# A two-layer graph network on one core: all seven column pieces of the first pass in fp32r, with GpSimd casting the last

## The chip, the cores and the metric

The kernel runs on one core of a Trainium2 chip. The metric is the device time of one execution in microseconds (us); 966.26 us is the median of three runs of the kernel before (964.35 to 967.14). Five engines work in parallel on the core, each through its own queue in program order: TensorE (PE in the profile, with PEld for its weight loads), VectorE (DVE), ScalarE (ACT), GpSimd (POOL) and SyncE (SP), which here issues most DMAs. Matmuls write to PSUM; all else lies in SBUF. fp32r is a 4-byte type that TensorE multiplies in one go[...].

## The reference

6250 nodes with 128 features each, 206,250 directed edges (100,000 drawn ones in both directions, and one loop per node), sorted by destination. Cut to what is computed:

```python
h = relu(layernorm(x))
feat = h * clip(out_degree, 1) ** -0.5
x = x + relu(segment_sum(feat[src], dst)) @ W0.T + b0            # first layer
h = relu(layernorm(x))
msg = h[src] @ W_msg.T + b_msg + edge_embed[edge_type]
x = x + gru_cell(segment_sum(msg, dst), h)                       # second layer
```

The two segment sums over edges are the bulk of it. All in float32.

## The kernel before, in words

**The idea.** The kernel does not gather rows. It builds the adjacency matrix (how many edges lead from each source to each destination) as small integers, exact in bf16, and takes each segment sum as a matmul of a node table with that matrix. Nodes are padded to 49 blocks of 128. The first pass (`by_matrix`, L757 to L909) builds the matrix in chunks of destination columns (`FRONT`: one of 128, then 24 of 256), uses each chunk at once for the first layer, and writes it to DRAM (`adj_d`). The second pass (L915 on) reads it back in columns of up to 512 for the second layer.

**The prologue** (L365 to L755) sorts edge data into windows by transposes and indirect DMAs on GpSimd's queue, takes layernorm statistics (`st`), counts degrees, and makes the table `tab1` of the first layer: seven pieces of seven source blocks each. A float32 table is split into terms that add up to it: piece 0 (`q < NARROW`) in three bf16 terms (`SPL`), the other six in two fp32r terms (`terms_of`, L722).

**The first pass**, one iteration of the loop at L856 for each chunk c, and one more at the end. An iteration does three things in turn, in 8 rounds of 32 columns (4 for the first chunk):
- *Building chunk c.* Every second round VectorE writes one-hot rows of 64 columns (`hots`: `hot_l`, `hot_c`, L334), one batch ahead of their use, in two buffers. Each round TensorE multiplies them (`ev`, L801, 32 small matmuls), and ScalarE copies the counts from PSUM into the chunk's matrix (`adj`, L810, two copies).
- *The sums of chunk c-1* (`sums`, L758; matmuls at L769): for each piece, block and term one matmul of 128x128 weights with 256 matrix columns. Piece 0 takes the bf16 matrix as it is: 7 blocks x 3 terms = 21 matmuls. Pieces 1 to 6 need the matrix in fp32r, so each is cast first (`cast`, L871): pieces 1, 3, 5 on ScalarE, 2, 4, 6 on VectorE, into three rotating buffers `wide1`; 6 x 7 x 2 = 84 matmuls. The 105 are spread over the 8 rounds (`ends`), 13 a round and 14 in the last. `cast_at` says in which round each cast is put: {0: (1, 2), 2: (3,), 3: (4,), 4: (5,), 5: (6,)}.
- *The dense end of chunk c-2* (`first_layer`, L815), a generator whose steps are taken in rounds 0, 2, 3 and 6: relu on ScalarE, the product with W0 on TensorE (L825), the residual sum on VectorE (L829, L830), statistics (L835, L836). Its last step, `late`, comes in round 2 of the next iteration: ScalarE's square root `rstd` (L838) and then VectorE's reciprocal and `sh` (L839, L840).

The order on TensorE, ScalarE and VectorE in this pass is the order of the program (`manual_schedule`, L786). GpSimd has no instruction in it.

The names that the steps below touch: `one_hot` L331, `hots` L341, `first_place` L361 (the memory of the first chunk's matrix, idle in the prologue, that also takes one early batch of one-hots), `st` L459, `tab1` L530, `inside` L623, `terms_of` L722, `sums` L758, `build` L790, `first_layer` L815, the loop L846 to L909.

Of the kernel before, what the change touches and what calls it, by code (L numbers as in the profile page):

```python
# [10 lines left out]
F32 = mybir.dt.float32  # L11
BF16 = mybir.dt.bfloat16
F32R = mybir.dt.float32r
# [3 lines left out]
ALU = mybir.AluOpType  # L17
# [4 lines left out]
P = 128  # L22
N = 6250
NB = 49
NP = NB * P
H = 128
# [5 lines left out]
CB = 7  # L32
NCH = NB // CB
# [3 lines left out]
HALF = P // 2  # L37
WP = 125
WB = 25
ROWS = 3  # L40
GB = 4
# [4 lines left out]
DC = 2 * P  # L46
FRONT = [(0, P)] + [(d, DC) for d in range(P, NP, DC)]
HP = 7
SPL = 3
LEVELS = 4  # L50
BY_ACT = (0, 2, 4, 6)
NARROW = 1
BACK = [(0, 3 * P)] + [(d, min(4 * P, NP - d)) for d in range(3 * P, NP, 4 * P)]


def spread(n, k):

    return [n * (i + 1) // k for i in range(k)]
# [200 lines left out]
def by_matrix(  # L259
# [22 lines left out]
    nc = tc.nc  # L282
# [70 lines left out]
    def run(steps, n):  # L353
        for _ in range(n):
            if next(steps, "end") == "end":
                return
# [4 lines left out]
    first_place = adj_odd.tile([P, NB, DC], BF16, name="adj").rearrange("p n d -> p (n d)")  # L361
# [3 lines left out]
    with tc.tile_pool(name="pro", bufs=1) as pro, tc.manual_schedule(engines={mybir.EngineType.DVE}):  # L365
# [90 lines left out]
            nc.vector.tensor_scalar(row, row, float(4 * HALF), None, op0=ALU.mult)  # L456


        st = pro.tile([P, NB, 6], F32, name="st")  # L459
        stats_left = iter(range(NB))  # L460

        def stats(n):
# [25 lines left out]
        for k0 in range(0, NT // P + 1, 4):  # L488
            k1 = min(k0 + 4, NT // P + 1)
            n = min(P, NT - k0 * P)  # L490
            for i, given in enumerate((dst_f, code_b, typ_b, low_b)):
                ps = pps.tile([P, 4, P], F32, name="turn")
                for k in range(k0, k1):
                    n = min(P, NT - k * P)
# [30 lines left out]
        nc.sync.dma_start(out=flat[NT : NT + 1, :], in_=far)  # L525
        look.close()


        tab1_p = early.enter_context(tc.tile_pool(name="tab1_p", bufs=1, side="right"))
        tab1 = [  # L530
            tab1_p.tile([P, SPL, CB, H], BF16, name=f"tab1_{q}")
            if q < NARROW
            else tab1_p.tile([P, 2, CB, H], F32R, name=f"tab1_{q}")
            for q in range(NCH)
        ]
        look = ExitStack()
        wnd = look.enter_context(tc.tile_pool(name="wnd", bufs=2))
# [70 lines left out]
        def fetch(b0_, nb):  # L608

            got = wnd.tile([P, GB, ROWS, 4, HALF], I16, name="got")  # L610
            for b in range(nb):
                nc.gpsimd.indirect_dma_start(  # L612
                    out=got[:, b].rearrange("p r f j -> p (r f j)"),
                    out_offset=None,
                    in_=edges_flat,
                    in_offset=bass.IndirectOffsetOnAxis(ap=row_i[:, b0_ + b : b0_ + b + 1], axis=0),
                )
            typ_of[b0_] = wnd.tile([P, GB * WP], BF16, name="typ")
            w0_ = b0_ * WP
            turns_ = {i: pps.tile([P, 4, P], F32, name="turn") for i in (1, 0, 2)}  # L620
            n = nb * ROWS
            g = got[:, :nb].rearrange("p b r f j -> p (b r) f j")
            inside = wnd.tile([P, 2, GB * ROWS, HALF], BF16, name="inside", bufs=1)  # L623
            fields = wnd.tile([P, GB * ROWS, 3, 2, HALF], BF16, name="fields")
            for d in range(2):
                nc.vector.tensor_tensor(
                    inside[:, d, :n].rearrange("p a (j t) -> p a j t", t=2),
                    g[:, :, 0, :].rearrange("p a (j t) -> p a j t", t=2),
                    mine[d][:, b0_ * ROWS : b0_ * ROWS + n].unsqueeze(2).to_broadcast([P, n, HALF // 2, 2]),
                    ALU.is_equal,  # L630
                )
            for d in range(2):
                nc.vector.tensor_tensor(  # L633
                    fields[:, :n, :, d, :],
                    g[:, :, 1:, :],
                    inside[:, d, :n].unsqueeze(2).to_broadcast([P, n, 3, HALF]),
                    ALU.mult,
                )
            for i in (1, 0, 2):
                for b in range(nb):  # L640
                    for r in range(ROWS):
                        nc.tensor.matmul(  # L642
                            turns_[i][:, b, :],
                            fields[:, b * ROWS + r, i].rearrange("p d j -> p (d j)"),
                            ident_b,
                            start=(r == 0),
                            stop=(r == ROWS - 1),
                        )
            for i in (1, 0, 2):
                ws = turns_[i][:, :nb, :WP]  # L650
                if i == 1:
                    nc.scalar.copy(typ_of[b0_][:, : nb * WP].rearrange("j (b p) -> j b p", p=WP), ws)
                else:
                    to = (code_t, None, lo_t)[i][:, w0_ : w0_ + nb * WP, :]
                    nc.scalar.copy(
                        to.rearrange("j (b p) t -> j b p t", p=WP), ws.unsqueeze(3).to_broadcast([P, nb, WP, 2])
                    )
# [64 lines left out]
        def terms_of(c):  # L722
            f, tab = f_of.pop(c), tab1[c]
            nc.vector.tensor_scalar(tab[:, 0], f, 0.0, None, op0=ALU.max)
            if c < NARROW:
                nc.vector.scalar_tensor_tensor(f, f, 0.0, tab[:, 0], op0=ALU.max, op1=ALU.subtract)
                nc.vector.tensor_copy(tab[:, 1], f)
                nc.vector.tensor_tensor(tab[:, 2], f, tab[:, 1], ALU.subtract)
            else:
                nc.vector.scalar_tensor_tensor(  # L730
                    tab[:, 1], f, 0.0, tab[:, 0].bitcast(F32), op0=ALU.max, op1=ALU.subtract
                )

        for i in range(NCH):
            if i >= 3:
# [46 lines left out]
    with tc.tile_pool(name="adj_even", bufs=1, reuse_waits="tile") as adj_even, tc.tile_pool(  # L782
        name="wide1", bufs=3, reuse_waits="tile"
    ) as wide1p, tc.tile_pool(
        name="ev_ps", bufs=3, space=PSUM, reuse_waits="tile"
# [58 lines left out]


        RUN = 32  # L846
        cast_at = {0: (1, 2), 2: (3,), 3: (4,), 4: (5,), 5: (6,)}
        TOTAL = (NARROW * SPL + (NCH - NARROW) * 2) * HP
        ROUNDS = DC // RUN
        batches = [d // 2 for d in range(0, NP, 2 * TW)]  # L850
        ready = early_hots
        made = len(ready)
        adjs = {}
        before, late = None, iter(())
        NC = len(FRONT)
        for c in range(NC + 1):  # L856
            d0, nd = FRONT[c] if c < NC else (NP, 0)
            acc, steps = None, iter(())
            wide = {}
            if c > 0:  # L860
                done = adjs.pop(c - 1)
                n = FRONT[c - 1][1]
                acc, steps = sums(
                    n, tab1, lambda q, done=done, wide=wide: wide[q] if q >= NARROW else done[:, q * HP : (q + 1) * HP]
                )
            if c < NC:
                adjs[c] = (adj_even if c % 2 else adj_odd).tile([P, NB, DC], BF16, name="adj") if c > 0 else adj_first
            rounds = nd // RUN if c < NC else ROUNDS
            ends = spread(TOTAL, rounds)

            def cast(q):  # L871
                wide[q] = wide1p.tile([P, HP, DC], F32R, name="wide1")
                make = nc.scalar.copy if (q - NARROW) % 2 == 0 else nc.vector.tensor_copy
                make(wide[q][:, :, :n], done[:, q * HP : (q + 1) * HP, :n])  # L874

            for r in range(rounds):
# [15 lines left out]
                for q in casts:  # L892
                    if r > 0:
                        cast(q)
                if before is not None and r in (0, 2, 3, 6):
                    run(before, 1)
                if r == 2:
                    run(late, 1)
                run(steps, ends[r] - (ends[r - 1] if r else 0))
            run(steps, TOTAL)  # L900
            late = before if before is not None else iter(())
            before = first_layer(c - 1, acc) if acc is not None else None
            if c < NC:
# [212 lines left out]
```

## Time and profile before

| what | us |
|---|---|
| median of 3 runs | 966.26 |
| profiled execution, its own time | 970.11 |
| its span in the profile | 968.3 |
| prologue, until the first sums on TensorE | 117 |
| first pass, until the second pass's sums start | 117 to about 571 |
| second pass | 571 to 968 |
| PE busy, of the span | 886.2 (92%) |
| DVE busy | 807.8 (83%) |
| ACT busy | 739.8 (76%) |
| POOL busy | 35.9 (4%), all of it in the prologue |

The profile is of one execution. A line of the groups names line, engine, operation, output<-input, shape and count, then busy time and the mean duration of one in ns, then the idle time of the engine before them and who ended it. A line of the timeline gives start, duration, engine, line, operation, operands and how many instructions were merged. Busy time is a union: a DVE or ACT instruction begins a little before the one ahead has left the pipeline, so durations add up to more than the busy time, and what an instruction costs is best taken from start to start. The ends of matmuls are modelled.

### The profile page before, as it was taken

Reading aid. Unit: us, or ns where it says so; the run is one execution under the profiler, and the core shown is the slowest. Engines: PE = TensorE matmul, PEld = TensorE weight load, DVE = VectorE, ACT = ScalarE, POOL = GpSimd, SP = SyncE. Lnnn points to the kernel's source line nnn. Section 1 sums busy time; section 2 is a strip of 40 time slices with the busy share of each in tenths; the row PEclk is TensorE's granted clock in tenths of the full one; section 3 lists DMA queues with packets and bytes.
Section 4 is the critical chain, followed back from the end, with each engine's and each line's share of the span. In section 5 each row is a group of like instructions: output and inputs, shape, how many; then the busy total and the mean of one; then the engine's idle time right before and its main releaser. Section 6 shows DMA issues by size and latency. Waiting matters only on the chain.

```text
span 968.3 us, 25145 instructions
## 1 busy us (share of the span) xinstructions
PE 886.2 (92%) x11049; PEld 735.5 (76%) x11049; DVE 807.8 (83%) x898; ACT 739.8 (76%) x1407; POOL 35.9 (4%) x73
## 2 busy tenths in 40 slices
PE   4356499999999999999999989999999999999995
PEld 3334399899899999999999878777777777777774
DVE  6969988999999999999999788987887778766753
ACT  3167889999999999999999995767577666667552
POOL 3540000000000000000000000000000000000000
PEclk9677599999999999999999999999999999999998
DMA  9430245575576576576476679877676677565530
GB/s 267 137 96 18 53 130 168 163 207 170 157 206 175 152 206 180 148 206 186 142 206 191 178 260 315 267 250 250 229 256 230 231 260 245 200 227 209 183 88 20
DMA packets 200296, 180.65 MB, mean 187 GB/s; under 512 B 10353, under 2 KB 188583, under 8 KB 200023
## 3 DMA queue, kind: packets, MB, share of 16 engines
q1 hardware_dynamic: 197938, 172.72, 57.5%
q0 software_dynamic: 1664, 4.95, 1.7%
q8 instruction: 88, 1.44, 0.6%
q10 hardware_dynamic: 576, 1.29, 0.4%
q14 instruction: 30, 0.25, 0.1%
HBM read 95.07 MB, written 83.87 MB: 185 GB/s over the span
## 4 chain that ended last, share of the span: by engine, by line
PE 74%; DVE 11%; ACT 7%; DMA 5%; issue 2%; POOL 1%; another core or an unknown queue 0%; SPq 0%; DVEq 0%; ACTq 0%
PE acc L769 52%; PE ev L801 10%; DMA piece<-adj_d 4%; DVE leave L1011 3%; PE turn L642 2%; PE gate L972 2%; PE acc L825 2%; PE gate L973 2%; DVE wide L1038 2%; ACT wide L1031 1%; ACT adj L810 1%; PE sums L671 1%; ACT f L935 1%; PE msg_ps L964 1%; PE tr L953 1%
## 5 line engine op out<-in xcount | busy, mean ns | idle before, releaser
L769 PE MATMUL acc<-wide,tab 128*128 128x256 f32 (+2 forms) x3374 | 600.1, 329 | 3.5 <-DVE wide L1038 3.4
L769 PEld LDWEIGHTS acc<-wide,tab 128*128 128x128 f32 x3374 | 492.0, 189 | 68.2 <-issue 17.7
L810 ACT CAST adj<-ev 128x784 bf16<-128x784 f32 x392 | 298.9, 820 | 30.6 <-PE ev L801 27.6
L1031 ACT ACTIVATE wide<-piece 128x512 fp32r<-128x512 bf16 (+1 forms) x336 | 201.0, 601 | 70.0 <-PE acc L769 64.0
L334 DVE TENSOR_TENSOR hot_l<-lo_t,iota 128x4096 bf16<-128x4096 bf16 x97 | 221.6, 2285 | 0.6 <-PE ev L801 0.5
L1011 DVE TENSOR_REDUCE leave<-piece 128x7 f32<-128x3584 bf16 (+2 forms) x43 | 154.9, 3602 | 47.2 <-DMA piece<-adj_d 47.2
L874 ACT CAST wide<-adj 128x1792 fp32r<-128x1792 bf16 (+1 forms) x75 | 125.2, 1669 | 0.8
L801 PE MATMUL ev<-hot_c,hot_l 64*128 64x49 bf16 x6208 | 114.2, 182 | 7.4 <-DVE hot_c L334 4.2
L801 PEld LDWEIGHTS <-hot_l 64*128 64x128 bf16 x6208 | 93.0, 93 | 36.0 <-issue 8.9
L334 DVE TENSOR_TENSOR hot_c<-code_t,iota 128x1600 bf16<-128x1600 bf16 x97 | 95.5, 985 | 0.0
L1038 DVE CAST wide<-piece 128x3584 fp32r<-128x3584 bf16 (+2 forms) x43 | 82.3, 1921 | 10.4 <-PE acc L769 10.4
L874 DVE CAST wide<-adj 128x1792 fp32r<-128x1792 bf16 (+1 forms) x75 | 81.0, 1079 | 8.7 <-ACT adj L810 7.9
L769 PE MATMUL acc<-adj,tab 128*128 128x256 bf16 x525 | 67.2, 277 | 0.5 <-ACT adj L810 0.5
L1031 ACT ACTIVATION_READ_ACCUMULATOR wide<-piece 128x1 f32 x336 | 63.2, 188 | 0.0
L769 PEld LDWEIGHTS <-tab 128*128 128x128 bf16 x525 | 48.1, 99 | 8.1 <-issue 0.6
L949 ACT COPY sum_sb<-acc 128x512 f32<-128x512 f32 (+2 forms) x13 | 7.3, 562 | 37.4 <-PE acc L769 37.4
L642 PE MATMUL turn<-ident_b,fields 128*128 128x128 bf16 x225 | 20.9, 280 | 15.4 <-DVE fields L633 15.4
L642 PEld LDWEIGHTS <-fields 128*128 128x128 bf16 x225 | 19.9, 131 | 16.1 <-issue 14.0
L612 POOL DMA_INDIRECT got<-flat,row_i x25 | 26.4, 1058 | 23.5 <-DVE m_dve L667 13.6
L972 PE MATMUL gate<-hT,whh_sb 128*128 128x512 f32 (+2 forms) x52 | 25.4, 570 | 1.2 <-DVE hT L961 1.2
L973 PE MATMUL gate<-msg,wih_sb 128*128 128x512 f32 (+2 forms) x52 | 25.3, 567 | 0.0
L980 ACT ACTIVATE rg<-gate,brz 128x512 f32<-128x512 f32 (+2 forms) x13 | 8.6, 664 | 20.0 <-PE gate L973 20.0
(160 smaller groups left out, 558.2 us busy)
## 6 DMA issues: line engine op xcount, KB each, us to landing
adj_d<-adj SPq DMA_DIRECT2D x24, 3136.0 KB
piece<-adj_d SPq DMA_DIRECT2D x77, 896.0 KB
piece<-adj_d SPq DMA_DIRECT2D x14, 672.0 KB
piece<-adj_d SPq DMA_DIRECT2D x7, 448.0 KB
out_dram<-res SPq DMA_DIRECT2D x11, 256.0 KB
xs<-in_x_dram SPq DMA_DIRECT2D x6, 448.0 KB
adj_d<-adj SPq DMA_DIRECT2D x1, 1568.0 KB
flat<-turned SPq DMA_DIRECT2D x3, 512.0 KB
```

The lines of the kernel that those rows point to most:

```text
L334: nc.vector.tensor_tensor(to.rearrange("p j (k t) -> p j k t", t=2), twice.unsqueeze(2).to_broadcast([P, n, m // 2, 2]), of[:, :m].rearran ...
L612: nc.gpsimd.indirect_dma_start(out=got[:, b].rearrange("p r f j -> p (r f j)"), out_offset=None, in_=edges_flat, in_offset=bass.IndirectOf ...
L642: nc.tensor.matmul(turns_[i][:, b, :], fields[:, b * ROWS + r, i].rearrange("p d j -> p (d j)"), ident_b, start=(r == 0), stop=(r == ROWS ...
L769: nc.tensor.matmul(acc[:, : 2 * P].rearrange("f (t n) -> f t n", t=2) if twice else acc[:, :nd], tab[:, s, i, :], a[:, i, :P].unsqueeze(1) ...
L801: nc.tensor.matmul(ps[:, d, j * NB : (j + 1) * NB], hot_l[half, t, :], hot_c[half, t, :NB], start=True, stop=True,)
L810: nc.scalar.copy(adj[:, :, part * 16 : (part + 1) * 16].rearrange("p n (j d) -> p n j d", d=2), ps[:, :, : 8 * NB].rearrange("p d (j n) -> ...
L874: make(wide[q][:, :, :n], done[:, q * HP : (q + 1) * HP, :n])
L972: nc.tensor.matmul(ps[:, :nd], whh_sb[:, cols], hT[:, :nd], start=True, stop=False)
L973: nc.tensor.matmul(ps[:, :nd], wih_sb[:, cols], msg[:, :nd], start=False, stop=True)
L1011: nc.vector.tensor_reduce(leave[:, q * HP : (q + 1) * HP, c], piece, AX.X, ALU.add)
L1031: nc.scalar.activation(pieces[q][:, i, :nd], piece[:, i, :nd], AF.Copy, accum_out=leave[:, q * HP + i, c : c + 1],)
L1038: nc.vector.tensor_copy(pieces[q][:, :, :nd], piece[:, :, :nd])
```

## The change

All seven pieces of `tab1` become two fp32r terms, so a chunk's sums are 7 x 7 x 2 = 98 matmuls, all on a cast matrix. The casts: pieces 1, 3, 5 on ScalarE as before; 0, 2, 4 on VectorE; piece 6 on GpSimd, into a buffer of its own (`wide1_last`, one buffer). The sums of a chunk begin in round 1 instead of round 0, and the 13 matmuls left after round 7 are run in round 0 of the next iteration (`rest`). The steps of `first_layer` move from rounds 0, 2, 3, 6 to 1, 3, 4, 6. To make room in SBUF, `st` and `inside` of the prologue are placed in `first_place`.

On the engines' queues: in each iteration VectorE's three casts stand in rounds 0, 1 and 3 (before: 0, 3 and 5), ScalarE's in 0, 2 and 4 as before. GpSimd gets 25 casts (one of 128x896, 24 of 128x1792 elements) behind its last prologue DMA. Each waits for ScalarE's last copies of the chunk and, by its single buffer, for the `rest` matmuls in round 0. ScalarE's first `adj` copy of an iteration now waits also for GpSimd's cast of the iteration before, which reads the same matrix buffer. VectorE has two instructions fewer in the prologue (of the four that made piece 0's terms, two are left). SP's queue is the same.

```diff
-NARROW = 1
...
-        st = pro.tile([P, NB, 6], F32, name="st")
+        st = first_place.bitcast(F32)[:, NB * P - NB * 6 :].rearrange("p (b s) -> p b s", s=6)
...
         tab1 = [
-            tab1_p.tile([P, SPL, CB, H], BF16, name=f"tab1_{q}")
-            if q < NARROW
-            else tab1_p.tile([P, 2, CB, H], F32R, name=f"tab1_{q}")
+            tab1_p.tile([P, 2, CB, H], F32R, name=f"tab1_{q}")
             for q in range(NCH)
         ]
...
-            inside = wnd.tile([P, 2, GB * ROWS, HALF], BF16, name="inside", bufs=1)
+            inside = first_place[:, 2 * NB * (P - 6) - 2 * GB * ROWS * HALF : 2 * NB * (P - 6)]
+            inside = inside.rearrange("p (d a j) -> p d a j", d=2, j=HALF)
...
             nc.vector.tensor_scalar(tab[:, 0], f, 0.0, None, op0=ALU.max)
-            if c < NARROW:
-                nc.vector.scalar_tensor_tensor(f, f, 0.0, tab[:, 0], op0=ALU.max, op1=ALU.subtract)
-                nc.vector.tensor_copy(tab[:, 1], f)
-                nc.vector.tensor_tensor(tab[:, 2], f, tab[:, 1], ALU.subtract)
-            else:
-                nc.vector.scalar_tensor_tensor(
-                    tab[:, 1], f, 0.0, tab[:, 0].bitcast(F32), op0=ALU.max, op1=ALU.subtract
-                )
+            nc.vector.scalar_tensor_tensor(
+                tab[:, 1], f, 0.0, tab[:, 0].bitcast(F32), op0=ALU.max, op1=ALU.subtract
+            )
...
-        cast_at = {0: (1, 2), 2: (3,), 3: (4,), 4: (5,), 5: (6,)}
-        TOTAL = (NARROW * SPL + (NCH - NARROW) * 2) * HP
+        cast_at = {0: (0, 1, NCH - 1), 1: (2,), 2: (3,), 3: (4,), 4: (5,)}
+        TOTAL = NCH * 2 * HP
...
-        before, late = None, iter(())
+        before, late, rest = None, iter(()), iter(())
...
-                    n, tab1, lambda q, done=done, wide=wide: wide[q] if q >= NARROW else done[:, q * HP : (q + 1) * HP]
+                    n, tab1, lambda q, wide=wide: wide[q]
...
-            ends = spread(TOTAL, rounds)
+            ends = [0, *spread(TOTAL, rounds)]
 
             def cast(q):
-                wide[q] = wide1p.tile([P, HP, DC], F32R, name="wide1")
-                make = nc.scalar.copy if (q - NARROW) % 2 == 0 else nc.vector.tensor_copy
+                if q == NCH - 1:
+                    wide[q] = wide1p.tile([P, HP, DC], F32R, name="wide1_last", bufs=1)
+                    make = nc.gpsimd.tensor_copy
+                else:
+                    wide[q] = wide1p.tile([P, HP, DC], F32R, name="wide1")
+                    make = nc.scalar.copy if q % 2 else nc.vector.tensor_copy
                 make(wide[q][:, :, :n], done[:, q * HP : (q + 1) * HP, :n])
...
-                if before is not None and r in (0, 2, 3, 6):
+                if r == 0:
+                    run(rest, TOTAL)
+                if before is not None and r in (1, 3, 4, 6):
                     run(before, 1)
                 if r == 2:
                     run(late, 1)
                 run(steps, ends[r] - (ends[r - 1] if r else 0))
-            run(steps, TOTAL)
+            if c == NC:
+                run(steps, TOTAL)
+            rest = steps
```

## The prediction, on record before the run

> **What bounds the kernel now.** I read the page first (shares, then the span in slices), then busy times by stretch of the first pass, then the timelines of TensorE (PE) and VectorE (DVE) inside one iteration, and last GpSimd's (POOL's) groups and timeline, since the change gives that engine new work. Part 2 of the page:
>
> ```profile
> PE   4356499999999999999999989999999999999995
> DVE  6969988999999999999999788987887778766753
> ACT  3167889999999999999999995767577666667552
> POOL 3540000000000000000000000000000000000000
> ```
>
> The change lies in the first pass, slices 5 to 23 (117 to 571 us). There three engines are at nine tenths, and POOL has nothing. Which of the three ends last is read from one iteration (from its first build matmul to the next one's), and from 19 of them; the columns are PE, PEld, DVE, ACT, POOL busy, then the granted clock, DMA share and GB/s:
>
> ```profile
> 172.33:190.60 18.27, 18.27 (x367) 16.57 (x367) 17.23 (x20) 17.11 (x22) 0.00 (x0) 1.00 0.60 178
> 172.33:519.46 347.13, 347.13 (x6946) 314.77 (x6947) 327.48 (x362) 325.21 (x400) 0.00 (x0) 1.00 0.62 178
> ```
>
> 347.13 / 19 = 18.27 us for an iteration, all of it PE: TensorE never waits, at full clock. DVE has 18.27 - 17.23 = 1.04 us free, ScalarE 18.27 - 17.11 = 1.16. So the pass is bound by TensorE, with two engines 6% behind it. TensorE's timeline at the end of the pass shows what its two kinds of matmul cost with nothing between them:
>
> ```profile
> 510.69 1.82 PE L769 MATMUL acc<-wide,tab 128*128 128x256 f32 x13
> ...
> 556.47 2.45 PE L769 MATMUL acc<-adj,tab 128*128 128x256 bf16 x21 [0.54 <-ACT adj L810]
> 558.68 0.84 PE L769 MATMUL acc<-wide,tab 128*128 128x256 f32 x5
> ...
> 559.73 9.72 PE L769 MATMUL acc<-wide,tab 128*128 128x256 f32 x79
> ```
>
> A group's time holds the modelled tail of its last matmul (a median of 0.285 us for fp32r). From start to start, bf16 takes (558.68 - 556.47) / 21 = 0.105 us, fp32r (9.72 - 0.285) / 78 = 0.121. DVE's order in the iteration:
>
> ```profile
> 172.05 1.06 DVE L874 CAST wide<-adj 128x1792 fp32r<-128x1792 bf16 x1
> 173.03 2.28 DVE L334 TENSOR_TENSOR hot_l<-lo_t,iota 128x4096 bf16<-128x4096 bf16 x1
> 175.23 0.98 DVE L334 TENSOR_TENSOR hot_c<-code_t,iota 128x1600 bf16<-128x1600 bf16 x1
> 176.13 2.28 DVE L334 TENSOR_TENSOR hot_l<-lo_t,iota 128x4096 bf16<-128x4096 bf16 x1
> 178.34 0.98 DVE L334 TENSOR_TENSOR hot_c<-code_t,iota 128x1600 bf16<-128x1600 bf16 x1
> 180.23 0.17 DVE L839 RECIPROCAL rstd<-rstd 128x2 f32<-128x2 f32 x1 [0.91 <-ACT rstd L838]
> ```
>
> Two things are to be seen. Nearly all of DVE's free 1.04 us is one wait, 0.91 us for ScalarE's rstd. And the one-hot batches come just in time: the batch that ends at 176.21 is used by round 2's matmuls, which TensorE starts at 176.47, 0.26 us later. If DVE is later there, TensorE waits at once.
>
> **TensorE's part of the change.** 105 matmuls become 98: 21 bf16 go (21 x 0.105 = 2.21 us) and 14 fp32r come (14 x 0.121 = 1.69): -0.51 us an iteration. The runs of sums stay eight between the builds (rounds 1 to 7 and the rest in round 0), so switching costs the same. 24 iterations with builds: -12.3 us, all on the path as long as TensorE is the bound. The 25th sum lies at the end of the pass, where ScalarE's L935 and its casts carry the chain; it saves nothing. A rule speaks for more: the Trainium skill, "TensorE: Matmul & The Clock Gate", section "Back-to-back issue gap", gives N/2.4 + 2.5 ns for a warm matmul whatever its type, 109 ns for 256 columns. By it seven fewer matmuls are -0.76 us, -18 us in all. The rows have two prices, 0.105 and 0.121, so I keep -12.3.
>
> **VectorE and ScalarE.** Each still makes three casts of the same size (0.98 us start to start on DVE); none is added or removed. DVE's go from rounds 0, 3, 5 to 0, 1, 3. Behind the one moved to round 1 stands the batch for round 4, whose lead is 181.44 - 179.32 = 2.1 us against 1 us more work: covered. The later batches have less in front of them and gain. The cast in round 3 waits for a buffer that TensorE frees four matmuls into that round, at worst some 0.3 us, inside DVE's slack. The other edges (first_layer a round later; ScalarE's first copy waiting for GpSimd's cast of an iteration ago) are hidden by a round of 2.2 us or more; without that cover they would cost 0 to 0.5 us an iteration. Sums that start a round later cost TensorE nothing in the middle, as the rest fills round 0. At the front one round of 13 matmuls (1.6 us) moves to the end of the pass, where ScalarE is the bound: between 0 and +1.6 us, and I take 0, since at 120.86 DVE waits 0.5 us for TensorE in that first iteration.
>
> **Prologue.** Piece 0's L727 and L728 go (71.80 to 73.46, 1.7 us of DVE). What follows on DVE has its data, but from 94 us on DVE waits for ScalarE (1.52 us at L703). Between 0 and -1.7 us: I take -0.9. `st` and `inside` in first_place are written and read by DVE alone, in order: nothing.
>
> **GpSimd's cast, the disputed cost.** 24 casts of 128x1792 and one half as long. No row shows one. The nearest:
>
> ```profile
> L551 POOL IOTA mine<- 128x150 int16 x2 | 1.4, 718 | 0.0
> ...
> L565 POOL MEMSET sel<- 128x531 bf16 x1 | 0.5, 534 | 0.0
> ...
> L440 POOL COPY pick<-ident 25x25 f32<-25x25 f32 x1 | 0.2, 197 | 0.0
> ```
>
> The memset writes 531 elements in 534 ns, 1.0 ns each; the copy of 25 elements shows what a read adds at the start, some 0.1 to 0.2 us. So a cast is about 1.8 + 0.15 = 1.95 us. Below: GpSimd's reference page in the skill ("GPSIMD Engine Reference", "Elementwise — side-by-side cycle accounting") has 1.03 cycles an element at best, an estimate of 1.5 us; above: its 4497 ns for a two-input add of 2048, an estimate of 3.9 us. The iota's 4.8 ns an element (8.6 us) is another kind of work. On GpSimd itself any of these is free: the buffer comes free at the end of round 0 and the piece is needed by the last matmul of round 7, some 13 us on.
>
> What it does to DVE is the question. A rule speaks against the change: the skill's "SBUF — State Buffer", section "SBUF: two separate sides", says that GpSimd shares a port pair with VectorE as an exclusive lock, held for a whole instruction by whoever starts first; it holds against DVE operations with two SBUF inputs when GpSimd reads SBUF, and against two-port copies. DVE's one-hots have two SBUF inputs and its casts are two-port copies: 12.4 + 2.9 of its 17.2 us. The trace can bear on it only in the prologue, first POOL, then DVE, then POOL:
>
> ```profile
> 43.55 1.43 POOL L612 DMA_INDIRECT got<-flat,row_i  x1 [0.30 <-issue]
> ```
> ```profile
> 42.82 2.62 DVE L633 TENSOR_TENSOR fields<-got,inside 128x2304 bf16<-128x2304 int16 x2
> ```
> ```profile
> 35.89 0.95 POOL L612 DMA_INDIRECT got<-flat,row_i  x1 [0.30 <-issue]
> ```
>
> GpSimd's DMA takes 0.95 us beside statistics and small operations, and 1.43 beside a two-input operation: they do get into each other's way. DVE's 2.62 us is the same without GpSimd beside it, so in these rows GpSimd pays. But [...]a cast that streams 1792 elements is not seen. By the rows alone DVE would lose 0 (the bound below; a gain is excluded, as nothing is taken from DVE), by the rule the whole cast. I take the rule: the cast becomes ready when round 0's 13 sums end, at about 174.6 on this iteration's clock, in the middle of hot_l, gets the port when hot_l ends at 175.3, and hot_c waits for it; it lands in the busiest stretch of DVE, not in the 0.91 us wait.
>
> **The sum.** DVE then needs 17.23 + 1.95 = 19.18 us an iteration against TensorE's 18.27 - 0.51 = 17.76; DVE is the bound, its wait for rstd is used up, and an iteration is 0.91 us longer than now. With 23.5 full casts: +21.4 us; with the prologue's -0.9: +20.5. The profiled execution (970.1, 1.8 of it outside the span of 968.3) would be 990.6; against the median of 966.26: 987. Next late is hot_c for round 2, then ev (L801).
>
> **Rivals.**
> A. *GpSimd streams beside DVE without holding it.* One mechanism, the port; it decides at 1.04 us: if an iteration costs DVE less than that, the kernel does not become slower. With nothing lost TensorE stays the bound, with DVE 17.23 and ScalarE 17.11 under 17.76: 966.3 - 12.3 - 0.9 = 953. For it: the DMA rows, where DVE's durations do not move. Against: the rule, and that GpSimd was slowed there.
> B. *The lock holds, and the cast runs at the two-input price.* 17.23 + 3.9 = 21.1, +2.86 x 23.5 - 0.9: 1032. For: bf16 to a 4-byte type is more than a memset. Against: one input only.
> C. *The change doesn't do what it says*: GpSimd never gets the port in time and TensorE waits for piece 6 in round 7. It needs a delay of 13 us; no DVE instruction is longer than 2.3, so I leave it 2 in 100, in B's part.
> D. *DVE loses about half the cast*, 0.9 to 1.2 us, and the gain is eaten: 963 to 970.
>
> **How the numbers follow.** The forecast 0.50, A 0.34, B with C 0.10, D 0.06. About 0.3% (3 us) is what a measurement of this kernel can tell from no change. Faster 0.34 (A), same 0.06 (D), slower 0.60 (forecast, B, C). The forecast's own range: a cast of 1.5 us with 0.2 of it in DVE's idle time gives 17.23 + 1.3, +0.26 x 23.5 - 0.9: 972; a cast of 3 us gives +46 - 0.9: 1012. The stated range must reach A, to 951 (the whole of the prologue's 1.7), and up to 1012; it leaves out most of B.
>
> **What would show it.** In the profile after: PE no longer full in a stretch of the first pass, idle before ev put down to DVE hot_c; some one-hots or DVE casts of 4 us instead of 2.3 or 1.1, beside a POOL cast; the wait for rstd gone. Steps: fp32r sums 98 an iteration at 0.121; a POOL cast near 1.95 us. I am wrong if the one-hots keep 2.28 and 0.98 us while GpSimd casts; then the iteration should be near 17.76.

## The result, and the profile after

The kernel after takes 980.7 us (median of 4 runs, 978.92 to 981.51), the kernel before beside it 966.21 (964.35 to 967.14): 1.015 times as long, interval 1.0129 to 1.0171, or +14.5 us. The forecast was 987, slower. The profiled execution took 980.43, with a span of 978.4.

Part 2 of the page of the kernel after, the same four rows as before:

```profile
PE   3366699999999999999999989999999999999995
DVE  6879989999999999999999978987887888766743
ACT  3287889898898889889888994765666757667562
POOL 3550001000100100010010000000000000000000
```

POOL now has a little work all through the first pass, and PE and DVE both read 9 there, so this view doesn't say which of them ends last. The stretch of one iteration does (columns as before: PE, PEld, DVE, ACT, POOL busy, clock, DMA share, GB/s):

```profile
242.18:261.17 18.99, 17.89 (x360) 16.39 (x360) 18.73 (x20) 17.05 (x22) 2.17 (x1) 1.00 0.58 172
```

An iteration takes 18.99 us instead of 18.27. TensorE, which was busy for all of it, now idles 18.99 - 17.89 = 1.10; VectorE has gone from 17.23 to 18.73 busy, with the same 20 instructions. VectorE's timeline inside this iteration, and GpSimd's:

```profile
242.01 1.09 DVE L872 CAST wide<-adj 128x1792 fp32r<-128x1792 bf16 x1
243.02 2.28 DVE L333 TENSOR_TENSOR hot_l<-lo_t,iota 128x4096 bf16<-128x4096 bf16 x1
245.22 2.46 DVE L333 TENSOR_TENSOR hot_c<-code_t,iota 128x1600 bf16<-128x1600 bf16 x1
...
250.81 0.98 DVE L333 TENSOR_TENSOR hot_c<-code_t,iota 128x1600 bf16<-128x1600 bf16 x1
251.72 0.15 DVE L831 RECIPROCAL rstd<-rstd 128x2 f32<-128x2 f32 x1
```
```profile
244.67 2.17 POOL L872 CAST wide_last<-adj 128x1792 fp32r<-128x1792 bf16 x1 [16.82 <-PE acc L761]
```

The extra time is one instruction: the hot_c that stands behind the first hot_l takes 2.46 us where its twin takes 0.98. GpSimd's cast is recorded from 244.67, in the middle of hot_l; hot_l keeps its 2.28 and hot_c waits until the cast is over. The reciprocal at 251.72 no longer waits for rstd.

Four groups from part 5 of the page (busy time, mean ns of one, then the idle time before them and its releaser):

```profile
L793 PE MATMUL ev<-hot_c,hot_l 64*128 64x49 bf16 x6208 | 114.0, 182 | 32.9 <-DVE hot_c L333 29.5
...
L872 POOL CAST wide_last<-adj 128x1792 fp32r<-128x1792 bf16 (+1 forms) x25 | 53.4, 2137 | 441.3 <-PE acc L761 405.4
L872 DVE CAST wide<-adj 128x1792 fp32r<-128x1792 bf16 (+1 forms) x75 | 82.9, 1106 | 9.9 <-ACT adj L802 7.2
...
L761 PE MATMUL acc<-wide_last,tab 128*128 128x256 f32 x350 | 51.9, 288 | 0.0
```

TensorE waits 29.5 us for hot_c; between 140 and 560 us it is 22 waits, 24.2 us in all, 1.10 each. In the third line VectorE's cast waits for ScalarE's last copies of the chunk. Nearly all of its 7.2 us lie in two early iterations (2.9) and in the last (4.3), and the kernel before has 7.9 in the same group; what becomes important below is a wait of the same kind of 0.1 to 0.2 us in every iteration. The last line is TensorE's sums on GpSimd's cast, with no idle time before them.

**The account of the pass.** From the first hot_l of the pass to the last is 447.6 us before (99.99 to 547.57) and 462.5 after (94.48 to 556.94): +14.9, which is the whole difference of the medians. (The two profiled executions are only 10.3 us apart, 970.11 and 980.43: in the second the pass happened to begin 5.5 us earlier.) It is not 23.5 times 0.73. Count the pass in 24 stretches of four hot_l. In the kernel before, those from about 125 and 144 us took 19.1 and 19.6 us with TensorE busy throughout (373 and 404 matmuls instead of 367), so VectorE had room there that it lacks later. The first three stretches together are 0.5 us shorter after than before; the 21 others are 0.73 longer: 15.3 - 0.5 = 14.8.

### The profile page after: what moved, and what is told of

It is laid out like the page before. It is cut to its first block, busy times and chain, and to the rows that moved or that the text cites. A ratio compares the mean times of both kernels' runs of the same rounds, so it can differ in the third digit from the quotient of the medians.

```text
span 978.4 us, 24889 instructions
## 1 busy us (share of the span) xinstructions
PE 875.7 (90%) x10874; PEld 732.0 (75%) x10874; DVE 841.7 (86%) x896; ACT 738.3 (75%) x1407; POOL 89.1 (9%) x98
## 3 DMA queue, kind: packets, MB, share of 16 engines
q10 hardware_dynamic: 576, 1.29, 0.4%
## 4 chain that ended last, share of the span: by engine, by line
PE 56%; DVE 24%; ACT 8%; DMA 5%; issue 4%; POOL 1%; SPq 0%; DVEq 0%; POOLq 0%; ACTq 0%
PE acc L761 38%; PE ev L793 7%; DVE hot_c L333 6%; DVE hot_l L333 5%; DMA piece<-adj_d 4%; ACT adj L802 4%; DVE leave L1013 3%; DVE wide L872 2%; PE gate L974 2%; PE gate L975 2%; DVE wide L1040 2%; PE acc L817 1%; ACT f L937 1%; DVE fields L630 1%; ACT wide L1033 1%
## 5 line engine op out<-in xcount | busy, mean ns | idle before, releaser
L802 ACT CAST adj<-ev 128x784 bf16<-128x784 f32 x392 | 294.5, 823 | 47.4 <-PE ev L793 47.1
L793 PE MATMUL ev<-hot_c,hot_l 64*128 64x49 bf16 x6208 | 114.0, 182 | 32.9 <-DVE hot_c L333 29.5
L333 DVE TENSOR_TENSOR hot_c<-code_t,iota 128x1600 bf16<-128x1600 bf16 x97 | 129.4, 1334 | 0.0
L872 POOL CAST wide_last<-adj 128x1792 fp32r<-128x1792 bf16 (+1 forms) x25 | 53.4, 2137 | 441.3 <-PE acc L761 405.4
L761 PE MATMUL acc<-wide_last,tab 128*128 128x256 f32 x350 | 51.9, 288 | 0.0
L761 PEld LDWEIGHTS acc<-wide_last,tab 128*128 128x128 f32 x350 | 44.8, 188 | 0.9
L608 POOL DMA_INDIRECT got<-flat,row_i x25 | 26.2, 1047 | 18.4 <-DVE m_dve L664 9.3
```

The costliest lines, as they stand in the source:

```text
L333: nc.vector.tensor_tensor(to.rearrange("p j (k t) -> p j k t", t=2), twice.unsqueeze(2).to_broadcast([P, n, m // 2, 2]), of[:, :m].rearran ...
L608: nc.gpsimd.indirect_dma_start(out=got[:, b].rearrange("p r f j -> p (r f j)"), out_offset=None, in_=edges_flat, in_offset=bass.IndirectOf ...
L761: nc.tensor.matmul(acc[:, : 2 * P].rearrange("f (t n) -> f t n", t=2) if twice else acc[:, :nd], tab[:, s, i, :], a[:, i, :P].unsqueeze(1) ...
L793: nc.tensor.matmul(ps[:, d, j * NB : (j + 1) * NB], hot_l[half, t, :], hot_c[half, t, :NB], start=True, stop=True,)
L802: nc.scalar.copy(adj[:, :, part * 16 : (part + 1) * 16].rearrange("p n (j d) -> p n j d", d=2), ps[:, :, : 8 * NB].rearrange("p d (j n) -> ...
```

## The experiments

The prediction's theory is called the *port theory* in the expectations: VectorE loses GpSimd's cast at the shared SBUF port, and VectorE becomes the bound. Against it stands the *order theory*: the new order of the sums and casts costs the time, with GpSimd harmless. A third idea came up on the way, the *ring* (or loop): no engine is full, but a chain of waits leads once round the engines and sets the period.

"Period" is the time from one iteration's first hot_l to the next one's. Ratios are to the kernel before, run on the same chip:

| kernel | made from | GpSimd in the pass | ratio (interval) | period |
|---|---|---|---|---|
| before | | none | 1 | 18.27 |
| after | | cast, 1792 elements | 1.0150 (1.0129 to 1.0171) | 18.99 |
| e1_no_cast | after | none | 0.9858 (0.9836 to 0.9880) | 17.84 |
| e2_pool_writes_only | after | memset, 1792 | 0.9856 (0.9839 to 0.9872) | 17.83 |
| e3_before_plus_cast | before | cast, 1792 | 1.0289 (1.0267 to 1.0312) | 19.56 |
| e4_no_gpsimd_alternating | after | none | 0.9998 (0.9986 to 1.0011) | 18.43, 18.27 |
| e5_cast_in_seven | after | 7 casts of 256 | 1.0005 (0.9995 to 1.0015) | 18.47 |
| e6_cast_beside_statistics | after | cast, 1792 | 1.0111 (1.0090 to 1.0132) | 18.83 |
| e7_beside_statistics_shared | after | cast, 1024 | 0.9979 (0.9969 to 0.9990) | 18.39 |
| e8_no_gpsimd_split | after | none | 0.9861 (0.9820 to 0.9902) | 17.88 |
| e9_cast_behind_hot_c | after | cast, 1792, later | 1.0039 (1.0023 to 1.0056) | 18.52 |
| e10_before_plus_cast_late | before | cast, 1792 | 1.0260 (1.0241 to 1.0279) | 19.47 |
| e11_four_blocks_behind_hot_c | after | cast, 1024, later | 0.9872 (0.9849 to 0.9895) | 17.88 |
| e12_plus_cast_loop_cut | before | cast, 1792 | 1.0090 (1.0057 to 1.0122) | 18.61 |

**No cast** (e1_no_cast). GpSimd does nothing; the sums of piece 6 run on piece 5's cast.

```diff
-        cast_at = {0: (0, 1, NCH - 1), 1: (2,), 2: (3,), 3: (4,), 4: (5,)}
+        cast_at = {0: (0, 1), 1: (2,), 2: (3,), 3: (4,), 4: (5, NCH - 1)}
...
-                    wide[q] = wide1p.tile([P, HP, DC], F32R, name="wide1_last", bufs=1)
-                    make = nc.gpsimd.tensor_copy
+                    wide[q] = wide[q - 1]
+                    return
```

> The changed kernel without GpSimd's cast: piece 6 is multiplied with the cast of piece 5, so the first layer's sums are not the reference's; everything else, the later start of the sums too, stays. Port theory (GpSimd's cast holds VectorE's hot_c up): hot_c is back at 0.98 us everywhere, VectorE needs 17.51 us an iteration start to start, TensorE is the bound again at 18.27 - 0.51 = 17.76, total 980.7 - 1.24 x 23.5 = about 951.5. Order theory (moving casts to rounds 0, 1, 3 and the sums a round later costs the time): an iteration stays at 18.9 to 19.0, total about 980.

954.52 us against 967.12. The order theory falls: the new order without the cast is 1.4% faster than before, and all hot_c take 0.98 us again. The period, 17.84, is the prediction's figure for TensorE (17.76) within 0.08.

**A GpSimd operation that only writes** (e2_pool_writes_only), of the same size in the same place, instead of the cast:

```diff
-                    make = nc.gpsimd.tensor_copy
+                    nc.gpsimd.memset(wide[q][:, :, :n].bitcast(F32), 1.0)
+                    return
```

> The changed kernel with GpSimd filling piece 6's buffer by a memset of the same 128x1792 4-byte elements instead of casting it (so piece 6's counts are replaced by ones). Same place in the order, same wait for TensorE, but GpSimd reads nothing from SBUF. If the lock on a two-input operation of VectorE only meets a GpSimd operation that reads (as the Trainium skill's SBUF page puts it): hot_c at 0.98, an iteration near 17.76, total about 952. If any GpSimd operation on the port blocks: hot_c longer by the memset's time less what runs beside hot_l, some 1.2 to 1.5 us, total 976 to 981. Order theory: about 980 in either case.

953.02 us: as if GpSimd were not there. GpSimd's and VectorE's timelines of this kernel:

```profile
255.20 1.60 POOL L868 MEMSET wide_last<- 128x1792 f32 x1 [16.23 <-PE acc L761]
```
```profile
255.78 0.98 DVE L333 TENSOR_TENSOR hot_c<-code_t,iota 128x1600 bf16<-128x1600 bf16 x1
```

The memset runs from 255.20 to 256.80, over the whole of this hot_c, and hot_c keeps 0.98 us. So it is not GpSimd being busy, nor its writes, that holds VectorE up. What the cast does besides is read SBUF.

**The kernel before with the cast alone** (e3_before_plus_cast): a GpSimd cast that nobody reads, in round 0; `st` and `inside` are moved as in the change to make room for it.

```diff
+                if q == 1:
+                    extra = wide1p.tile([P, HP, DC], F32R, name="wide1_last", bufs=1)
+                    nc.gpsimd.tensor_copy(extra[:, :, :n], done[:, (NCH - 1) * HP :, :n])
```

> The kernel before (105 matmuls, its own rounds) plus one thing: in round 0 GpSimd casts piece 6 of each chunk into a buffer that nobody reads (st and inside placed as in the change, for room). Port theory: VectorE needs 17.51 + 1.5 = 19.0 us an iteration against TensorE's 18.27, so about +0.73 x 23.5 = +17: 983; less if the cast, free of the wait for TensorE, falls into other instructions, but never below the 1.5 us minus 0.76 of VectorE's slack. Order theory: nothing, 966.

994.63 us against 967.12: +27.5, the right direction and too much. GpSimd's and VectorE's timelines:

```profile
247.62 2.63 POOL L878 CAST wide_last<-adj 128x1792 fp32r<-128x1792 bf16 x1 [16.93 <-ACT adj L811]
```
```profile
247.65 1.06 DVE L875 CAST wide<-adj 128x1792 fp32r<-128x1792 bf16 x1
248.63 3.77 DVE L334 TENSOR_TENSOR hot_l<-lo_t,iota 128x4096 bf16<-128x4096 bf16 x1
...
257.11 0.17 DVE L840 RECIPROCAL rstd<-rstd 128x2 f32<-128x2 f32 x1 [0.71 <-ACT rstd L839]
```

GpSimd's record begins with VectorE's cast, yet that cast keeps its 1.06 us; hot_l behind it goes from 2.28 to 3.77, +1.49, the same loss as in the kernel after. So GpSimd's 2.63 us are 1.0 of waiting for the cast ahead of it and 1.6 of its own, as the 2.17 above are 0.57 of waiting for hot_l (244.67 to about 245.24) and 1.60. But an iteration became 1.29 us longer while VectorE still idles 0.71 for rstd: VectorE isn't the bound here, and 17.23 + 1.49 = 18.72 is far from 19.56. This contradicted the port theory's sum and asked for another bound.

**Piece 6 to VectorE and ScalarE by turns** (e4_no_gpsimd_alternating): in round 5, one iteration on the one, the next on the other, four buffers in `wide1`.

```diff
-        cast_at = {0: (0, 1, NCH - 1), 1: (2,), 2: (3,), 3: (4,), 4: (5,)}
+        cast_at = {0: (0, 1), 1: (2,), 2: (3,), 3: (4,), 4: (5,), 5: (NCH - 1,)}
...
+                by_act = c % 2 if q == NCH - 1 else q % 2
+                make = nc.scalar.copy if by_act else nc.vector.tensor_copy
```

> The change without GpSimd: piece 6 is cast in round 5 by VectorE in one iteration and by ScalarE in the next, from a pool of four rotating buffers. Port theory: VectorE 17.51 + 0.5 = 18.0 us an iteration on average, ScalarE 17.05 + 0.8 = 17.85, TensorE 17.76; an iteration near 18.0, less than before's 18.27: 966.2 - 0.27 x 23.5 - 1.7 (prologue) = about 958. Order theory: no better than 975.

966.71 us, no change; a miss. The iterations take 18.43 and 18.27 us in turn. (The expectation of e8 below has 19.4 and 17.3: these are counted from the last hot_l of an iteration, which has VectorE's cast of piece 6 ahead of it every other time.) Where VectorE makes the cast, it has no gap: 18.27 is all its own work. Where ScalarE makes it, the cast stands ahead of its last copies; VectorE waits 1.04 us for these, and TensorE 0.39.

```profile
274.49 1.09 DVE L869 CAST wide<-adj 128x1792 fp32r<-128x1792 bf16 x1 [1.04 <-ACT adj L802]
```

Averaged over two iterations every engine has room, but each iteration is held up by the one that has the cast, and the other's room doesn't help.

**The cast in seven pieces** (e5_cast_in_seven), one of 256 elements for each block:

```diff
-                    make = nc.gpsimd.tensor_copy
+                    for i in range(HP):
+                        nc.gpsimd.tensor_copy(wide[q][:, i, :n], done[:, q * HP + i, :n])
+                    return
```

> The changed kernel with GpSimd's cast of piece 6 split into seven instructions of 256 elements, at the same place in the order. If the port is held for one instruction at a time: each small cast (0.23 us of work, 0.3 with its start) slips in behind one of VectorE's operations and delays the next by 0.15 to 0.3, no one-hot longer than 2.6 or 1.3 us, sum over an iteration 1.0 to 1.6 us (those that meet statistics, reciprocal or the PSUM add cost nothing), an iteration 18.5 to 19.1, total 969 to 983. If the port is held until GpSimd's queue is empty: one hot_c is longer by 1.5 to 2 us as before, total 980 to 990.

970.02 us against 969.80. VectorE's timeline:

```profile
244.08 1.18 DVE L333 TENSOR_TENSOR hot_c<-code_t,iota 128x1600 bf16<-128x1600 bf16 x1
245.19 1.28 DVE L874 CAST wide<-adj 128x1792 fp32r<-128x1792 bf16 x1
246.39 2.47 DVE L333 TENSOR_TENSOR hot_l<-lo_t,iota 128x4096 bf16<-128x4096 bf16 x1
```

Six times in an iteration a small cast slips in ahead of a VectorE operation and costs it about 0.20 us: 6 x 0.20 = 1.2. So the port goes to the waiting engine at the end of each instruction, and cutting the cast up spreads the loss without removing it.

**Two kernels that were meant to move the cast** (e6_cast_beside_statistics, e7_beside_statistics_shared) to round 6, beside VectorE's small statistics, behind a copy of one element that waits for the last hot_c; in the second, GpSimd casts four blocks and ScalarE three.

```diff
+                    if len(ready) > 1:
+                        seen = work.tile([P, 1], BF16, name="seen", bufs=1)
+                        nc.gpsimd.tensor_copy(seen, ready[-1][1][:, TW - 1, CODES - 1 :])
```

> The changed kernel with GpSimd's whole cast moved to round 6, behind a one-element GpSimd copy that waits for round 6's hot_c, so that it starts when VectorE begins the four statistics instructions (1.02 us[...]); piece 6 is multiplied only in round 0 of the next iteration, rounds 1 to 7 take 12 matmuls each. Port theory: hot_c stays at 0.98; of the 1.6 us cast some 0.3 to 0.6 us still delay VectorE's cast in round 0, part of which it waits anyway; VectorE needs 17.5 + 0.1 to 0.6 an iteration, total 955 to 963. If GpSimd's cast costs VectorE its 1.5 us wherever it stands: 976 to 981.

> As the one before, but GpSimd casts four of piece 6's seven blocks (0.92 us, inside the statistics) and ScalarE the other three in round 6 (0.85 us). Port theory: VectorE loses nothing and needs 17.5, ScalarE 17.05 + 0.85 = 17.9, TensorE 17.83: total 954 to 958. If GpSimd's cast costs VectorE its length wherever it stands: VectorE 18.3, total 964 or more.

Both missed their forecasts (955 to 963 and 954 to 958; 981.37 and 968.14 came), and neither says anything of the place: GpSimd's order isn't written by hand in this pass, and the cast was put ahead of the small copy, so it stayed where it was (hot_c at 2.47 us in the first). What is left of the first is that rounds 1 to 7 take 12 matmuls each and 14 are left over: 18.83 instead of 18.99. The second still gives a size: with 1024 elements hot_c loses 0.85 us, with 1792 it loses 1.49.

**No GpSimd, the piece split within each iteration** (e8_no_gpsimd_split): in round 6 VectorE casts four blocks and ScalarE three; four buffers in `wide1`.

```diff
+                    nc.vector.tensor_copy(wide[q][:, :4, :n], done[:, q * HP : q * HP + 4, :n])
+                    nc.scalar.copy(wide[q][:, 4:, :n], done[:, q * HP + 4 :, :n])
+                    return
```

> The change without GpSimd, piece 6 shared in each iteration: in round 6 VectorE casts four of its blocks (0.6 us) and ScalarE three (0.85), four rotating buffers. The alternating version gained nothing, with iterations of 19.4 and 17.3 us in turn. If that was because each engine was overloaded every other iteration: VectorE 18.1 and ScalarE 17.9 in every iteration give 18.1, total 966.2 - 0.17 x 23.5 - 2 = about 960. If an engine's slack cannot be used at all in this pass: 966 or more.

957.99 us against 969.80, period 17.88, with no wait of TensorE or VectorE to be seen in an iteration. VectorE at its end:

```profile
255.47 0.69 DVE L868 CAST wide<-adj 128x1024 fp32r<-128x1024 bf16 x1
256.07 0.29 DVE L827 BATCH_NORM_STATS2 st<-xs 128x6 f32<-128x128 f32 x1
...
256.79 0.18 DVE L828 BATCH_NORM_AGGREGATE mv<-st 128x2 f32<-128x6 f32 x1
256.89 1.06 DVE L873 CAST wide<-adj 128x1792 fp32r<-128x1792 bf16 x1
```

This gives VectorE's own need: 17.88 less the 0.60 us (start to start) of the added part cast is 17.28. It also shows that a cast with nothing to wait for starts 0.10 us behind the last statistics instruction.

**The cast really moved** (e9_cast_behind_hot_c, and e11_four_blocks_behind_hot_c with the split of e7). The copy of one element now writes into the cast's own buffer, so the cast must follow it:

```diff
+                    if len(ready) > 1:
+                        nc.gpsimd.tensor_copy(wide[q][:, 0, :1], ready[-1][1][:, TW - 1, CODES - 1 :])
```

> The move to round 6 again, this time in fact: the one-element GpSimd copy of round 6's hot_c goes into the cast's own buffer, so the cast cannot be put ahead of it (in the two runs before it was, and stayed at its old place right behind the rest of the sums). Port theory: the cast starts some 0.35 us behind hot_c and ends 1.95 behind it; VectorE's statistics (0.82 us start to start) run beside it at their usual length, and only its next cast waits, for 0.8 to 1.1 us; hot_c stays at 0.98. VectorE then needs 17.28 + 0.8 to 1.1 = 18.1 to 18.4 us an iteration, total 960 to 968. If the cast costs VectorE 1.5 us wherever it stands: 19.0 us an iteration, 980.

> The same with GpSimd casting four of the seven blocks (0.92 us) and ScalarE three (0.75 us start to start). Port theory: the cast ends 1.27 us behind hot_c, VectorE loses at most 0.45 and needs 17.28 + 0.45 = 17.73, ScalarE 17.05 + 0.75 = 17.8, TensorE 17.83: an iteration 17.85 to 18.0, total 955 to 959, level with the version without GpSimd (958). If place does not matter: 18.1 or more, as with the four blocks at the old place (18.39): 963 to 968.

The first takes 975.77 us against 971.75, the second 959.18. GpSimd and VectorE in the first:

```profile
257.61 1.68 POOL L874 CAST wide_last<-adj 128x1792 fp32r<-128x1792 bf16 x1
```
```profile
257.12 0.29 DVE L827 BATCH_NORM_STATS2 st<-xs 128x6 f32<-128x128 f32 x1
...
258.01 2.23 DVE L874 CAST wide<-adj 128x1792 fp32r<-128x1792 bf16 x1
```

The statistics beside the cast keep their durations; the loss begins with the next VectorE cast, a copy, 2.23 us instead of 1.08. It is 1.15 us instead of 1.49, and with four blocks 0.32 (that cast takes 1.40). The first is above its forecast (18.1 to 18.4 us an iteration, 960 to 968 in all), because the loss is more than the 0.8 to 1.1 us that were expected: VectorE works through the whole iteration without a wait, and 17.28 + 1.15 = 18.43 is near the measured 18.52. TensorE also waits 0.6 us for `wide_last` in round 0, but it has 18.52 - 17.84 = 0.68 to spare.

**Where the kernel before with a cast loses its time.** Two runs were to tell two ideas apart: that VectorE's wait for rstd in e3 closes the ring (e10_before_plus_cast_late moves that step, `late`, from round 2 to round 3), or that the ring goes through VectorE's cast of piece 2, which stands ahead of round 0's one-hots and waits for ScalarE's last copies (e12_plus_cast_loop_cut keeps e10's edit and moves that cast behind them as well).

```diff
-                if r == 2:
+                if r == 3:
                     run(late, 1)
```

> The kernel before with GpSimd's unread cast (it took 19.56 us an iteration, not the 19.0 forecast) and one more edit: late, the step with ScalarE's square root and VectorE's two operations on it, is taken in round 3 instead of round 2. In the run before VectorE still waited 0.71 us for that root, since a late hot_c makes TensorE, then ScalarE, then the root late too. If that loop is the missing 0.5 us: the wait goes, 18.9 to 19.1 an iteration, total 980 to 985. If not: 19.5, 994.

```diff
-                    if r == 0:
+                    if r == 0 and q != 2:
                         cast(q)
...
-                    if r > 0:
+                    if r > 0 or q == 2:
                         cast(q)
```

> The kernel before with GpSimd's unread cast and late in round 3 (19.46 us an iteration, no better than without the move of late), and one more edit: VectorE's cast of round 0 (piece 2) stands behind round 0's one-hots instead of ahead of them. Loop theory: the 19.5 us are a ring through three engines: VectorE's cast waits for ScalarE's last adj copy of the chunk, round 0's one-hots stand behind it (with GpSimd's 1.5 us in them), TensorE waits for those in round 2 and needs 11.8 us to round 7, whose counts ScalarE then copies: 5.7 + 11.8 + 2.0 = 19.5. With the cast behind the one-hots the ring is cut; what is left is VectorE's own 17.28 + 1.49 = 18.8 us, 19.1 with what is left of the wait for rstd: 12 to 20 us over the kernel before on the same chip. If the ring is not the cause: still 25 to 28 us over it.

The first gave 997.36 us against 971.75 (+25.6): the wait for rstd fell from 0.71 to 0.34 us, and the period only from 19.56 to 19.47. That looks as if rstd were not the cause, but the traces say something else. VectorE, TensorE and VectorE again in e3, then VectorE in e10:

```profile
271.87 0.98 DVE L334 TENSOR_TENSOR hot_c<-code_t,iota 128x1600 bf16<-128x1600 bf16 x1
```
```profile
272.90 0.58 PE L802 MATMUL ev<-hot_c,hot_l 64*128 64x49 bf16 x32 [1.22 <-DVE hot_c L334]
```
```profile
276.66 0.17 DVE L840 RECIPROCAL rstd<-rstd 128x2 f32<-128x2 f32 x1 [0.71 <-ACT rstd L839]
```
```profile
253.11 1.09 DVE L875 CAST wide<-adj 128x1792 fp32r<-128x1792 bf16 x1 [0.15 <-ACT adj L811]
```

In e3 VectorE has no wait from the reciprocal at 257.11 to the end of the hot_c at 272.85 (15.74 us); ev follows at 272.90 (0.05), and behind it ScalarE's two copies, its cast and its root, until the next reciprocal at 276.66 (3.76): 19.55, the whole period. So e3's ring does go through rstd. In e10 VectorE's cast waits for ScalarE's copies, which it did not in e3: now the other ring is the bound. The two differ by 0.09 us, and opening one alone leaves the other.

The second gave 974.89 against 967.17 (+7.7): with the same cast still there, 0.86 us of e10's 19.47 are gone, 0.18 of it because hot_l loses less. The total is less than the forecast 12 to 20 us over the kernel before. GpSimd's and VectorE's timelines:

```profile
261.85 1.68 POOL L878 CAST wide_last<-adj 128x1792 fp32r<-128x1792 bf16 x1 [16.93 <-ACT adj L811]
```
```profile
262.07 3.59 DVE L334 TENSOR_TENSOR hot_l<-lo_t,iota 128x4096 bf16<-128x4096 bf16 x1
```

GpSimd has a start of 0.2 us, so hot_l loses 1.31 where the forecast had 1.49; VectorE waits for nothing any more, and 17.28 + 1.31 = 18.59 is the measured period of 18.61. With both rings open, the port theory's sum is right.

## Why the prediction was right, and where its sizes were off

**The mechanism** was the predicted one, in the predicted place: the cast becomes ready within hot_l, starts when hot_l ends, and hot_c waits for it; round 2's ev is late next, and the wait for rstd is gone. The rule that it rested on, in the Trainium skill's "SBUF — State Buffer", section "SBUF: two separate sides", is what the runs show part by part: whoever starts first keeps the port for a whole instruction (e3, +1.49 us; e5, 6 x 0.20), two-input operations are held up by a GpSimd operation that reads SBUF and not by one that only writes it (e2, 0), and VectorE's casts are held up too (e9, +1.15). Rival A (no lock, 953) is what e1 and e2 measure, 954.52 and 953.02: the sum for the case without the lock held, and that case is not the one that came. The stated range reached down to that rival, so it is these rows, not the time alone, that decide. Rivals B and D fall with the measured loss of 1.49 us, rival C with the 0.0 us of idle time before the sums on `wide_last`.

**TensorE's step**: 17.76 forecast, 17.84 measured without the cast. By the one price for both types that the prediction took from the Trainium skill ("TensorE: Matmul & The Clock Gate", section "Back-to-back issue gap"), it would have been 18.27 - 0.76 = 17.51. That section gives the formula for an isolated matmul, not for a stream with weight loads like this one; the measurement stands with the two prices of the rows.

**The cast's size** was the term that was off. Forecast 1.95 us, all of it lost by VectorE; measured 1.60 to 1.68 of work and 1.49 lost. The memset row that I scaled (531 elements in 534 ns, 1.0 ns each) comes out too high: at 1792 elements a memset takes 1.60 us (e2), 0.89 ns an element, and a cast with nothing in its way 1.68 (e9), so reading adds at most 0.08, not 0.15. The lower of the prediction's two estimates, 1.5, was nearer. VectorE then needs 17.28 + 1.49 = 18.77, not 19.18.

**A bound that the prediction did not have.** The period is 18.99, not 18.77. The remaining 0.22 is a ring, the one through VectorE's cast. Follow it in the kernel after, on TensorE, ScalarE and VectorE:

```profile
247.75 0.58 PE L793 MATMUL ev<-hot_c,hot_l 64*128 64x49 bf16 x32 [1.10 <-DVE hot_c L333]
...
259.02 0.58 PE L793 MATMUL ev<-hot_c,hot_l 64*128 64x49 bf16 x32
```
```profile
259.44 1.53 ACT L802 CAST adj<-ev 128x784 bf16<-128x784 f32 x2 [0.57 <-PE ev L793]
```
```profile
260.70 0.18 DVE L828 BATCH_NORM_AGGREGATE mv<-st 128x2 f32<-128x6 f32 x1
261.00 1.09 DVE L872 CAST wide<-adj 128x1792 fp32r<-128x1792 bf16 x1
```

VectorE's cast at 242.01, hot_l and the held-up hot_c end at 247.68 (5.67 us). TensorE waits for that and starts round 2's ev at 247.75; from there it has no gap until round 7's ev at 259.02 (11.27). ScalarE copies its counts until 260.97, and VectorE's next cast, which waits for them, starts at 261.00: 0.30 us behind the last statistics instruction, where e8 shows 0.10 for a cast that waits for nothing. 5.67 + 0.07 + 11.27 + 1.98 = 18.99. That the pieces add up to the period is no proof by itself; what shows the ring is that each of them begins as soon as the one before it ends, while each engine is idle somewhere.

Run e6 bears this out by accident. Its rounds have one matmul less between round 2's ev and round 7's, which are 11.11 us apart there instead of 11.27. The period falls by the same 0.16, to 18.83, although hot_c is held up as long as before (2.47), and VectorE's cast starts 0.13 behind the statistics: VectorE's own work is now the bound. In the kernel before with the cast, opening this ring took most of 0.86 us off an iteration (e10 to e12). For the kernel after, opening it altogether was not tried.

**The sum.** 0.91 an iteration was forecast, 0.73 came: -0.46 for the cast, +0.05 for VectorE's own need, +0.22 for the ring. That the total is so near is in part luck: the cast was taken too long and the ring was not seen, and the two errors go opposite ways. And the 0.73 was not paid 23.5 times but in effect some 20 times (14.9 / 0.73), since two early stretches had room. The prologue's -0.9 can't be told from the scatter: the pass begins anywhere from 92.4 to 101.1 us in the profiles of this study, on average at 98.3 in the four with piece 0's old terms (before, e3, e10, e12) and at 96.2 in the ten without them, but not all on one chip; on the chip of e1 to e4 it is 95.0 with them (e3) and 92.4 to 94.3 without. What is shown is that the pass alone accounts for the difference of the medians.

**A version that beats both**: e8 (0.986) and, level with it within the intervals, e11 (0.987). Seven pieces in fp32r are worth 1.4% as soon as piece 6's cast is shared so that no engine's need passes TensorE's 17.84.

## What to carry to other kernels

Work for an idle GpSimd is priced by what it holds, not by what it computes: here, if it reads SBUF while VectorE runs two-input operations or casts, its duration goes into VectorE's sum; if it only writes beside two-input operations (e2), or runs beside statistics (e9), it does not. When several engines are within a few per cent of the bound, add up the chains of waits once round the loop too: one can be longer than any engine's own work (18.99 against 18.77), a second can stand right behind it (19.47 behind 19.56), and an engine's room can't be averaged over two iterations (e4).

## What the runs showed of the hardware

- GpSimd's cast of 128x1792 from bf16 to fp32r takes 1.60 to 1.68 us of work, little more than a memset of 1792 4-byte elements (1.60, e2). Its record includes the wait for the port: 2.17 and 2.63 us for the same cast in the kernel after and e3, and 1.68 in e9 and e12, where nothing stood in its way.
- VectorE goes on a little before GpSimd's record ends. The operation behind loses what is left of that record when it would have started, less 0.13 to 0.15 us: 1.49 of 1.62 (e3), 1.28 - 1.15 in e9, 1.46 - 1.31 in e12.
- VectorE's statistics (0.29 and 0.18 us) were not slowed at all beside a running GpSimd cast (e9).
